# Layer 1's half tile taken by row in pairs, layer 2's loads issued in layer 1, and layer 1's last tiles closed between layer 2's first projections

## The chip, the cores and the metric

The kernel runs on one core of one Trainium2 chip, in one launch. The metric is the device time of that launch in microseconds (us); smaller is better. The core has five engines that run side by side, each through its own queue in order: PE (TensorE: matmuls and the loads of their weights, PEld), DVE (VectorE), ACT (ScalarE), POOL (GpSimd) and SP, whose queue here issues DMA transfers. Matmuls write to PSUM, which has eight banks of 512 fp32 columns by 128 partitions; DVE and ACT take the results out.

## The reference

Four layers follow each other on `x` of shape (4, 56, 56, 256), all in fp32, each after a normalisation and with the input added back: a 7x7 local attention (layer 0), a graph step over all tokens of an image (layer 1), a neighbourhood attention in two dilations (layer 2) and a shifted-window attention (layer 3). The change concerns layer 1, of which the reference is, cut to what matters:

```python
xn = x / maximum(norm(x, axis=-1), EPS)
A  = einsum('bnc,cc,bmc->bnm', xn, W_adj, xn)      # n = m = 3136 tokens
A  = exp(5.0 * (A - max(A))) * (1 - eye(n))
A  = A / sum(abs(A))
rowsum = sum(A);  xW = x @ W_aff.T
diff = rowsum * (xW + b_aff) - (A @ x) @ W_aff.T
y = (diff - mean(diff)) * rsqrt(var(diff) + LN_EPS) * ln_gamma + ln_beta
y = where(y > 0, y, 0.01 * y)
```

Only the diagonal of `W_adj` is used, so `A` before its row normalisation is symmetric: one block of exponentials serves the rows of one tile and, transposed, the rows of the other.

## The kernel before, in words

Activations lie channels first in DRAM, one buffer for each layer's input. `direct_blocks` runs `layer0` to `layer3` one after the other. Each layer opens its own memory pools (`early`, `big`, `pool`, `brief`, and one for PSUM), on alternate sides of SBUF, and closes them at its end. The program's order is an order of the text for PE in layer 1 and for all engines in layer 3 (`manual_schedule`); elsewhere a scheduler orders each engine's queue by its own estimate, and may lift an instruction out of a later layer as far as its memory and data allow.

**Layer 1** treats one image after the other. Its 3136 tokens make 24 tiles of 128 and a last one of 64 (tile 24, padded with zeros to 128). For each image the kernel keeps in SBUF `xnT` (unit-length tokens, channels on the partitions), `xw` (tokens times `W_aff`, with a column of -1 that yields the row sums) and `acc` (sums for tiles by column).

- `tokens` (L1346 to L1395) fills these four tiles (a chunk) at a time: `load` (DMA, normalise at L939, square on ACT at L1360), `lengths` (L1368), `values` (L1381, taken out by `evac` at L952 and L954) and `unit_length` (L1389, then L1391 on DVE). For the first image all seven chunks go through at once, loads two chunks ahead. For the next image each chunk is replaced while the present one no longer needs it, its steps spread between the units by a list `small`.
- The main loop goes through **units**: for each row block j = 0..24, groups of up to four tiles i >= j. A unit is `logits` (L1409: two accumulating matmuls of up to 512 columns; L1412: exp on ACT; on the diagonal a mask on POOL, L1414), `transposed` (L1423 on PE, L1426 on ACT) and `products`: for each tile a row product into `ps_o` (L1437, summed over the whole row block) and a column product into one of two `ps_v` buffers (L1442), which DVE adds to `acc` (L1446; the first time it copies, L1444). PE's order is: transposes of this unit, logits of the next, products of this one. An image has 91 units.
- When a row block is complete, `finish` (L1466 to L1489) adds both sums on DVE (L1473) and runs the layer normalisation over DVE and POOL; some units later `add` transposes the result back (L1494), adds it to the residual `xr` (L1502), takes statistics (L894) and writes the block out (L1505). After the last unit all remaining `add` steps run in a row.

**Layer 2** begins with `load(0)` (L1585), its weights `w_qkv` (L881), a bias table of 6.2 MB in two transfers (L1591), the exponential of half of that table in one ACT instruction (L1592), and then, for three row pieces, `prepare` (normalise, L939; the load of the next piece) and `project_rows` (value tiles L982, keys and queries L945). Its x tiles have two buffers. Value tiles go to DRAM and come back gathered (L1688) for the attention, whose logits (L1071) use 32 rows of the array each and whose products (L1100) use 32 columns each.

Of the kernel before, what the change touches and what calls it, by code (L numbers as in the profile page):

```python
# [31 lines left out]
NIMG = 4  # L32
# [798 lines left out]
def direct_blocks(ctx: ExitStack, tc: tile.TileContext, d: dict, watch):  # L831
# [499 lines left out]
    def layer1(early, big, pool, brief):  # L1331
        NB = -(-T // P)
        real = lambda i: min(P, T - i * P)
        nonlocal m_bufs
        m_bufs, ps_a = 1, ps_m
        w_aff = weight(early, "waff", C)
        acc = big.tile([P, NB, C + 1], FP, name="acc")
        xnT = big.tile([P, CC, NB * P], FP, name="xnT")
        xw = big.tile([P, NB, C + 1], FP, name="xw")
# [3 lines left out]
        nc.vector.memset(xw[T % P:, NB - 1, :], 0.0)  # L1343
        nc.vector.memset(xnT[:, :, T:], 0.0)

        def tokens(b, c, ps_a=ps_m):  # L1346

            tiles = range(4 * c, min(4 * c + 4, NB))
            n = sum(real(t) for t in tiles)
            k, m = real(tiles[0]), len(tiles)  # L1350
            box = {}

            def load():
                x = early.tile([P, CC, 512], FP, tag="x", name="x1")
                nc.sync.dma_start(out=x[:, :, :n], in_=tokens_of(1, b, 4 * c * P, n))
                x1 = box["x"] = early.tile([P, CC, 512], FP, tag="xn", name="xn1")
                sq = box["sq"] = early.tile([P, CC, 512], FP, tag="sq", name="sq", bufs=1)
                for h in range(CC):
                    normalise(x1[:, h, :n], x[:, h, :n], known(1, b), h)
                nc.scalar.activation(sq[:, :, :n], x1[:, :, :n], AF.Square)  # L1360

            def lengths():
                pm, sq = ps_a(), box["sq"]
                rn = early.tile([P, 4, 1], FP, tag="rn", name="rn")
                dg = box["dg"] = early.tile([P, 4, P], FP, tag="dg", name="dg", bufs=1)
                for i, t in enumerate(tiles):
                    for h in range(CC):
                        nc.tensor.matmul(pm[:k, i:i + 1], lhsT=sq[:, h, i * P:i * P + k], rhs=ones[:, 0:1],  # L1368
                                         start=(h == 0), stop=(h == CC - 1))
                nc.vector.tensor_scalar_max(rn[:k, :m, 0], pm[:k, :m], TINY * TINY)  # L1370
                nc.gpsimd.tensor_tensor(rn[:k, :m, 0], rn[:k, :m, 0], mhalf[:k, 0:1].to_broadcast([k, m]), ALU.pow)
                nc.gpsimd.tensor_tensor(
                    dg[:k, :m, :k], ident[:k, :k].rearrange("p (o q) -> p o q", o=1).to_broadcast([k, m, k]),
                    rn[:k, :m, :].to_broadcast([k, m, k]), ALU.mult)

            def values(i0):
                pm = ps_a()
                mm = min(2, m - i0)
                for i in range(i0, i0 + mm):
                    for h in range(CC):  # L1380
                        nc.tensor.matmul(pm[:k, (i - i0) * C:(i - i0 + 1) * C], lhsT=box["x"][:, h, i * P:i * P + k],  # L1381
                                         rhs=w_aff[:, h, :], start=(h == 0), stop=(h == CC - 1))
                evac(i0 // 2, xw[:k, 4 * c + i0:4 * c + i0 + mm, :C],
                     pm[:k, :mm * C].rearrange("p (a b) -> p a b", b=C))

            def unit_length():

                pm = ps_a()
                nc.tensor.matmul(pm[:, :n].rearrange("p (m k) -> p m k", k=k), lhsT=ones[:k, :], rhs=box["dg"][:k, :m, :k],  # L1389
                                 start=True, stop=True)  # L1390
                nc.vector.tensor_tensor(xnT[:, :, 4 * c * P:4 * c * P + n], box["x"][:, :, :n],  # L1391
                                        pm[:, :n].rearrange("p (o k) -> p o k", o=1).to_broadcast([P, CC, n]), ALU.mult)

            return [load, lengths] + [lambda i=i: values(i) for i in range(0, m, 2)] + [unit_length]

        xd, out, xr = {}, {}, {}

# [6 lines left out]
        def logits(b, j, first, last):  # L1404
# [10 lines left out]
            return e  # L1415

# [12 lines left out]
        def products(b, j, first, last, e, at):  # L1429
# [10 lines left out]
            def by_column(i):  # L1440
                pv = psum_tile("v", 2)
                nc.tensor.matmul(pv[:, :C + 1], lhsT=e[:, col(i)], rhs=xw[:, j, :], start=True, stop=True)  # L1442
                if j == 0:
                    nc.vector.tensor_copy(acc[:, i, :], pv[:, :C + 1])  # L1444
                else:
                    nc.vector.tensor_tensor(acc[:, i, :], acc[:, i, :], pv[:, :C + 1], ALU.add)  # L1446
# [10 lines left out]

        def residual(b, c):

            if (b, c) not in xr and c < NCH:  # L1460
                xr[b, c] = pool.tile([P, CC, CH], FP, tag="xr", name="xr1", bufs=3)
                nc.sync.dma_start(out=xr[b, c], in_=tokens_of(1, b, c * CH, CH))
            return xr.get((b, c))

        def finish(b, j):

            n = real(j)
            y = pool.tile([P, C + 1], FP, tag="y", name="y", bufs=5)
# [3 lines left out]
            if j:  # L1472
                nc.vector.tensor_tensor(y[:n], out[j][:n, :C + 1], acc[:n, j, :], ALU.add)  # L1473
            else:
                nc.vector.tensor_copy(y[:n], out[j][:n, :C + 1])
# [15 lines left out]
            def add():  # L1491
                pt = ps_a()
# [4 lines left out]
                while t0 < j * P + n:  # L1497
# [5 lines left out]
                    if t1 == (c + 1) * CH:  # L1503
# [7 lines left out]
        NC4 = -(-NB // 4)  # L1511
        units = [(b, j, i, min(i + 4, NB)) for b in range(NIMG) for j in range(NB) for i in range(j, NB, 4)]
        turn = iter(range(4 * NC4))
        fresh = [tokens(0, c, lambda: psum_tile(*(("v", 2), ("o", 2), ("t", 1), ("s", 2))[next(turn) % 4])) for c in range(NC4)]
        for c in range(2):
            fresh[c].pop(0)()
        for c in range(NC4):
            for step in fresh[c]:
                step()
            if c + 2 < NC4:  # L1520
                fresh[c + 2].pop(0)()
        scaled(0)
        e = logits(*units[0])
# [9 lines left out]
        def there(b, tile):  # L1533

            for item in [a for a in small if a[2] == (b, tile // 4)]:
# [3 lines left out]
        def replace(b, c):  # L1539
            load, *steps = tokens(b, c)  # L1540
            load()
            at = sum(a[2] is not None for a in small)
            small[at:at] = [(done + 8, step, (b, c)) for step in steps]

        for k, w in enumerate(units):
            b, j, first, last = w
            if first == j:
                residual(b, j * P // CH)
                residual(b, j * P // CH + 1)
                if b + 1 < NIMG and j % 4 == 2 and j >= 6:  # L1550
                    replace(b + 1, j // 4 - 1)
                if b + 1 < NIMG and j == NB - 1:
                    replace(b + 1, NC4 - 2)
                if b and j == 0:
                    replace(b, NC4 - 1)
            small_step()
            at = transposed(*w, e)
            if k + 2 < len(units) and units[k + 2][1] == units[k + 2][2]:
                scaled(units[k + 2][1])
            if k + 1 < len(units):  # L1560
                there(units[k + 1][0], units[k + 1][3] - 1)
                ahead = logits(*units[k + 1])
            small_step()
            products(*w, e, at)
            done += last - first
            if last == NB:
                small.append((done + 6, finish(b, j), None))
            e = ahead
        for _, step, _ in small:
            step()  # L1570
# [5 lines left out]
    def layer2(early, big, pool, brief):  # L1576
        nonlocal m_bufs
        m_bufs = 2
        (types1, w1), (types2, w2) = window_types(S), window_types(G2)
        xs, xns, q, attns, ahead = {}, {}, {}, {}, []  # L1580
# [5 lines left out]

        load(0)
        w_qkv = weight(early, "wqkv2", 3 * C)
        bias = early.tile([P, 4, w1 + w2], FP, name="bias2", bufs=1)
        for a in (1, 0):  # L1590
            nc.sync.dma_start(out=bias[:, 2 * a:2 * a + 2, :], in_=d["bias2"][:, 2 * a:2 * a + 2, :])  # L1591
        nc.scalar.activation(bias[:, 2:4, :], bias[:, 2:4, :], AF.Exp)  # L1592
# [164 lines left out]
        for i in range(3):  # L1757
            prepare(i + 1)
            for step in project_rows(i):
                step()  # L1760
        attend_pairs(pool, stream())
# [193 lines left out]
    for l, layer in enumerate((layer0, layer1, layer2, layer3)):  # L1955
        side = "left" if l % 2 == 0 else "right"
        with tc.tile_pool(name=f"d{l}e", bufs=2, side=side, reuse_waits="tile") as early, \
                tc.tile_pool(name=f"d{l}", bufs=1, side=side, reuse_waits="tile") as big, \
                tc.tile_pool(name=f"d{l}w", bufs=2, side=side, reuse_waits="tile") as pool, \
                tc.tile_pool(name=f"d{l}l", bufs=2, side=side, reuse_waits="tile") as brief, \  # L1960
                tc.tile_pool(name=f"dpsum{l}", bufs=2, space=PSUM, reuse_waits="tile") as ps:
            E = mybir.EngineType
            fixed = {layer1: {E.PE}, layer3: {E.PE, E.DVE, E.Activation, E.Pool}}.get(layer)
            order = tc.manual_schedule(engines=fixed) if fixed else nullcontext()
            with order:
                layer(early, big, pool, brief)
# [99 lines left out]
```

## Time and profile before

| | us |
|---|---|
| three timed runs | 4103.39, 4103.79, 4105.45 (median 4103.79) |
| the profiled execution | 4092.52 |
| its span, first to last instruction | 4090.7 |
| mean granted PE clock | 0.979 |
| layer 1's steady part | about 850 to 2826 |
| layer 2's first projection | starts at 2845.9 |

The profile has, beside its page, the order of time of every engine, what each waited for, and busy times by stretch. Times in it count from the start of the span. "Busy" of PE is the union of its matmuls, each shown with its latency, so that the distance between two starts is the better price of a matmul. A merged row (x4) stands for that many instructions in a row; a matmul of fp32 operands appears as two, a transposition as one. The granted clock is the share of its full rate that PE was given.

### The profile page before, as it was taken

What the parts mean: (1) busy time and instruction counts of PE and PEld (TensorE: products, weight loads), DVE (VectorE), ACT (ScalarE), POOL (GpSimd) and SP (SyncE); (2) the same over time, 40 slices, a digit from 0 to 9 for tenths busy, and PEclk for the clock granted to TensorE, in tenths of its full rate; (3) what the DMA queues carried; (4) which work ended last, traced back from release to release, by engine and by line L of the source; (5) the groups of instructions that cost most, each with busy time, mean ns of one, the idle gap of its engine ahead of it and who ended that gap; (6) DMA issues with size and microseconds to landing.
All of it is one profiled execution on the core that took longest, in us unless ns stands there. A gap on an engine that the chain in (4) does not pass through costs nothing. (4 is left out here: it accounts for less than half of the span.)

```text
span 4090.7 us, 92322 instructions
## 1 busy us (share of the span) xinstructions
PE 3889.7 (95%) x39031; PEld 2778.1 (68%) x39031; DVE 2369.5 (58%) x4445; ACT 1377.7 (34%) x2890; POOL 1741.9 (43%) x1883
## 2 busy tenths in 40 slices
PE   7899999899999999999999999997999999999998
PEld 4566666577777677776777767775676766666665
DVE  6777777634445444454344543444688877666665
ACT  3445555322222122222222212222555555444443
POOL 2576767621123211242112421123677777554544
PEclk9899999899999999999999999998999999999999
DMA  7344333210000100001000000002344443322221
GB/s 259 101 136 126 116 116 104 90 32 10 15 15 24 34 10 15 15 24 34 10 15 15 23 23 9 10 19 108 108 135 124 131 118 111 108 72 73 73 75 63
DMA packets 239986, 275.88 MB, mean 67 GB/s; under 512 B 22342, under 2 KB 231912, under 8 KB 239080
## 3 DMA queue, kind: packets, MB, share of 16 engines
q1 hardware_dynamic: 239274, 269.80, 21.0%
q8 instruction: 309, 5.06, 0.5%
q14 instruction: 115, 0.94, 0.1%
q10 hardware_dynamic: 288, 0.08, 0.0%
HBM read 190.29 MB, written 79.53 MB: 66 GB/s over the span
## 5 line engine op out<-in xcount | busy, mean ns | idle before, releaser
L1446 DVE TENSOR_TENSOR acc<-acc,ps_v 128x257 f32<-128x257 f32 x1104 | 457.7, 421 | 679.2 <-PE ps_v L1442 676.5
L1442 PE MATMUL ps_v<-xw,e 128*128 128x257 f32 x2400 | 666.6, 382 | 27.2 <-DVE acc L1446 17.2
L1437 PE MATMUL ps_o<-xw,at 128*128 128x257 f32 x2400 | 663.2, 380 | 0.0
L1409 PE MATMUL ps_s<-xnT,xd 128*128 128x512 f32 (+3 forms) x1456 | 622.9, 550 | 5.1 <-DVE xnT L1391 5.1
L1442 PEld LDWEIGHTS ps_v<-xw,e 128*128 128x128 f32 x2400 | 445.0, 189 | 193.2 <-issue 91.8
L1426 ACT COPY at<-ps_t 128x512 f32<-128x512 f32 (+3 forms) x360 | 184.8, 513 | 1053.7 <-PE ps_t L1423 1053.7
L1091 POOL TENSOR_TENSOR b<-e 126x336 f32<-126x336 f32 (+5 forms) x512 | 499.7, 997 | 11.6 <-ACT e L1079 3.6
L1437 PEld LDWEIGHTS ps_o<-xw,at 128*128 128x128 f32 x2400 | 455.9, 190 | 65.5
L1402 POOL TENSOR_SCALAR xd<-xnT,vec 128x128 f32<-128x128 f32 x200 | 122.2, 622 | 707.4 <-PE ps_s L1409 705.6
L945 PE MATMUL ps_m<-xn,w_wqkv 128*128 128x392 f32 x1024 | 380.1, 505 | 2.7 <-DVE xr L1729 2.7
L1082 POOL TENSOR_TENSOR e<-e,m0t 126x672 f32<-126x672 f32 (+3 forms) x128 | 239.3, 1870 | 271.1 <-ACT e L1081 229.6
L1409 PEld LDWEIGHTS ps_s<-xnT,xd 128*128 128x128 f32 x1456 | 245.1, 191 | 155.6 <-issue 138.8
L1082 POOL TENSOR_TENSOR e<-e,bias 119x784 f32<-119x784 f32 (+5 forms) x128 | 244.6, 1911 | 202.0 <-ACT e L1081 200.8
L1412 ACT ACTIVATE e<-ps_s 128x512 f32<-128x512 f32 (+3 forms) x364 | 200.8, 552 | 376.7 <-PE ps_s L1409 376.0
L1003 ACT ACTIVATE no<-rs 128x168 f32<-128x168 f32 (+2 forms) x256 | 93.8, 367 | 596.2 <-DVE rs L1694 271.7
L945 PEld LDWEIGHTS ps_m<-xn,w_wqkv 128*128 128x128 f32 x1024 | 189.4, 192 | 126.1 <-ACT pr L1922 17.5
L1100 PEld LDWEIGHTS ps_o<-e,vp 124*32 124x32 f32 (+3 forms) x8192 | 176.9, 111 | 142.3 <-issue 94.8
L1100 PE MATMUL ps_o<-e,vp 124*32 124x112 f32 (+3 forms) x8192 | 239.5, 254 | 6.1 <-POOL e L1082 4.5
L939 DVE TENSOR_SCALAR xn<-x,gst 128x28 f32<-128x28 f32 (+5 forms) x368 | 206.1, 614 | 56.4 <-PE ps_m L945 27.7
L1079 ACT ACTIVATE e<-e 126x672 f32<-126x672 f32 (+5 forms) x256 | 219.5, 857 | 19.2 <-DVE e L1078 6.2
L1694 DVE RECIPROCAL rs<-ps_o 128x196 f32<-128x196 f32 (+2 forms) x128 | 176.0, 1375 | 78.8 <-PE ps_o L1100 78.3
L1032 POOL TENSOR_TENSOR e<-e,m3l 98x784 f32<-98x784 f32 x64 | 118.2, 1847 | 236.1 <-ACT e L1029 236.1
(169 smaller groups left out, 6176.6 us busy)
## 6 DMA issues: line engine op xcount, KB each, us to landing
x<-xr SPq DMA_DIRECT2D x64, 392.0 KB
x<-in_x SPq DMA_DIRECT2D x53, 448.0 KB
xr<-x SPq DMA_DIRECT2D x60, 392.0 KB
x<-x SPq DMA_DIRECT2D x60, 392.0 KB
vd<-v SPq DMA_DIRECT2D x48, 384.0 KB
xr<-in_x SPq DMA_DIRECT2D x32, 392.0 KB
xr<-x SPq DMA_DIRECT2D x28, 448.0 KB
x<-xr SPq DMA_DIRECT2D x28, 448.0 KB
```

What stands on the lines that cost most here:

```text
L939: nc.vector.tensor_scalar(dst, src, gst[:, h, 0:1], gst[:, h, 1:2], ALU.subtract, ALU.mult)
L945: nc.tensor.matmul(pm[:, :n], lhsT=w[:, h, col:col + P], rhs=rhs(h), start=(h == 0), stop=(h == CC - 1))
L1079: nc.scalar.activation(ev, ev, AF.Exp)
L1082: nc.gpsimd.tensor_tensor(parts(ev), parts(ev), w["emask"], ALU.mult)
L1091: nc.gpsimd.tensor_tensor(w["b"][a][:nk, :, :2 * nq].rearrange("p h (i c) -> p h i c", i=2), ev[:, :, :, 0, :], ev[:, :, :, 1, :], ALU.add)
L1100: nc.tensor.matmul(w["o"](k, i)[j * HD:(j + 1) * HD], lhsT=ones[:nk, :HD] if k else v(j, u), rhs=w["b"][j // 2][:nk, j % 2, i * nq:(i + 1) ...
L1409: nc.tensor.matmul(s[:, :n], lhsT=xd[j][:, h, :], rhs=xnT[:, h, first * P:last * P], start=(h == 0), stop=(h == CC - 1))
L1412: nc.scalar.activation(e[:, :n], s[:, :n], AF.Exp, scale=5.0)
L1426: nc.scalar.copy(at[:, sl], pt[:, sl])
L1437: nc.tensor.matmul(out[j][:, :C + 1], lhsT=e[:, col(i)] if i == j else at[:, col(i)], rhs=xw[:, i, :], start=(i == j), stop=(i == NB - 1))
L1442: nc.tensor.matmul(pv[:, :C + 1], lhsT=e[:, col(i)], rhs=xw[:, j, :], start=True, stop=True)
L1446: nc.vector.tensor_tensor(acc[:, i, :], acc[:, i, :], pv[:, :C + 1], ALU.add)
```

## The change

**The half tile.** Tile 24 leaves the row blocks: j and i now run over 24 tiles, and the blocks of an image make 84 units. The half tile is treated as a row of its own, in three units (q = 0, 1, 2) of eight tiles each. The last chunk of tokens loads the 64 tokens twice, so that they stand on partitions 0 to 63 and 64 to 127, and POOL scales them into `xdr`. In a unit, the logits of the 64 tokens with tiles 8q..8q+3 go to partitions 0 to 63 of `ps_s`, those with 8q+4..8q+7 to partitions 64 to 127; one exp, four transposes and one copy serve both halves. Then, four times, two column products that read 64 partitions each, into both `ps_v` buffers, and two row products that write 64 partitions each of one `ps_o`; `racc` sums the row products over the three units. For the first image units 0 and 1 come first and unit 2 after block 0; for a later image units 0 and 1 come after blocks 20 and 21 of the image before, unit 2 after its own block 0. A column sum is copied into `acc` when touched first, on DVE or (second half) on ACT, and added by DVE otherwise.

**Chunks.** The squares are written over the loaded x instead of into a buffer of their own, and the chunks of the next image are replaced at blocks 3, 6, 10, 14, 18, 20 and 22.

**The layer boundary.** Layer 2's `early` pool is opened before layer 1's pools. `layer2_ahead`, with `load(0)`, `w_qkv`, the bias table and its exponential in six pieces, is called inside layer 1 (text position: third image, block 8; the queues' own order sets when it is issued). The pool with `y` and `xr` (`late`) lives on into layer 2, and the `add` steps still open at the end of layer 1 are returned and run one by one after each step of layer 2's second and third `project_rows`.

```diff
+        def rest_logits(q):
+            s = psum_tile("s", 2)
+            for a in range(2):
+                for h in range(CC):
+                    nc.tensor.matmul(s[a * REST:(a + 1) * REST, :], lhsT=xdr[:, h, a * REST:(a + 1) * REST],
+                                     rhs=xnT[:, h, (2 * q + a) * 512:(2 * q + a + 1) * 512], ...)
+            e = pool.tile([P, 512], FP, tag="e", name="e1", bufs=3)
+            nc.scalar.activation(e, s, AF.Exp, scale=5.0)
...
+        def rest_products(b, q, e, own, at):
+            po = psum_tile("o", 2)
+            for i in range(4):
+                pv = [psum_tile("v", 2) for a in range(2)]
+                for a in range(2):
+                    half = slice(a * REST, (a + 1) * REST)
+                    nc.tensor.matmul(pv[a][:, :C + 1], lhsT=e[half, i * P:(i + 1) * P], rhs=xw[half, NB, :], ...)
+                for a in range(2):
+                    add_up(b, 8 * q + 4 * a + i, pv[a], (nc.vector.tensor_copy, nc.scalar.copy)[a])
+                for a in range(2):
+                    nc.tensor.matmul(po[a * REST:(a + 1) * REST, :C + 1], lhsT=at[:, i * P + a * REST:i * P + (a + 1) * REST],
+                                     rhs=xw[:, 8 * q + 4 * a + i, :], ...)
+            if own is not None:
+                nc.tensor.matmul(po[:REST, :C + 1], lhsT=own, rhs=xw[:REST, NB, :], start=False, stop=True)
...
-                sq = box["sq"] = early.tile([P, CC, 512], FP, tag="sq", name="sq", bufs=1)
+                sq = box["sq"] = x
...
+                if c == NC4:
+                    for h in range(CC):
+                        nc.gpsimd.tensor_scalar_mul(xdr[:, h, :], xnT[:, h, NB * P:], adj[:, h:h + 1])
...
-        for _, step, _ in small:
-            step()
+        return [step for _, step, _ in small]
...
+        def exponential(h, i):
+            part = bias[:, h, i * (w1 + w2) // 3:(i + 1) * (w1 + w2) // 3]
+            nc.scalar.activation(part, part, AF.Exp)
...
             for step in project_rows(i):
                 step()
+                if i and last_steps:
+                    last_steps.pop(0)()
```

In the changed kernel the matmuls of the half tile stand at L1443 (logits), L1451 and L1479 (its own 64 by 64 block), L1462 (transposes), L1472 (column products) and L1476 (row products); full tiles at L1421, L1491, L1505 and L1510, the adds to `acc` at L1433, the closing transposes at L1562.

## The prediction

> **What bounds the kernel now.** I read the page's first two parts first, for the engine that is always busy, then the order of time on TensorE (PE) for the price of one step, then the stretches around the end of layer 1.
>
> ```profile
> PE 3889.7 (95%) x39031; PEld 2778.1 (68%) x39031; DVE 2369.5 (58%) x4445; ACT 1377.7 (34%) x2890; POOL 1741.9 (43%) x1883
> ...
> PE   7899999899999999999999999997999999999998
> ...
> PEclk9899999899999999999999999998999999999999
> ```
>
> PE is busy 95% of the span, in every slice but the first and the one after layer 1; no other engine passes 58%. In layer 1 (850 to 2826 us) PE is busy 1935.2 of 1976 us, DVE 860. What leaves PE there leaves the time. Now PE alone, in one full unit of layer 1 (start, length, engine, line; "x4" counts merged instructions):
>
> ```profile
> 1410.44 0.60 PE L1423 MATMUL ps_t<-ident,e 128*128 128x128 f32 x4
> 1410.87 1.88 PE L1409 MATMUL ps_s<-xnT,xd 128*128 128x512 f32 x4
> 1412.59 1.03 PE L1442 MATMUL ps_v<-xw,e 128*128 128x257 f32 x4
> 1413.46 0.60 PE L1437 MATMUL ps_o<-xw,at 128*128 128x257 f32 x2
> ...
> 1415.19 1.03 PE L1437 MATMUL ps_o<-xw,at 128*128 128x257 f32 x4
> 1416.06 0.49 PE L1423 MATMUL ps_t<-ident,e 128*128 128x128 f32 x3
> ```
>
> Starts, not lengths, give the price, because matmuls overlap by their latency. 1410.44 to 1416.06 is 5.62 us for four tile pairs, 1.405 us each: transposition 0.108, logits 0.43, column product 0.433, row product 0.433. Each matmul is two passes, each costing 0.843 ns a column (0.43 us for 512). Units follow with no gap.
>
> The end of layer 1 (length, then busy time with counts for PE, PEld, DVE, ACT and POOL, then the granted PE clock and DMA):
>
> ```profile
> 2826.00:2846.00 20.00, 2.25 (x9) 1.11 (x9) 11.25 (x35) 0.20 (x1) 6.70 (x10) 0.58 0.52 183
> 2846.00:2857.00 11.00, 10.57 (x36) 6.49 (x36) 1.12 (x2) 4.34 (x10) 0.00 (x0) 0.83 0.98 422
> 2857.00:2865.00 8.00, 0.00 (x0) 0.00 (x0) 0.27 (x1) 4.11 (x2) 0.00 (x0) 0.69 0.77 281
> ```
>
> PE does 2.25 us of work in 20, then layer 2's first projection, then nothing for 8, while the clock falls to 0.58. The waits name it: closing transposes for y (5.0 us) and xr (5.7), the w_qkv transfer (7.1), the second xn (8.7).
>
> **Part 1, the half tile.** Before, tile 24 costs one pair in each of 24 row blocks and its own: 24 x 1.405 + 0.88 = 34.6 us an image. After, three units an image take eight tiles each, in 64-row or 64-column halves. In line: logits 8 passes of 512 (3.46), four transposes (0.43), products 32 passes of 257 (6.93), three times over, plus 0.65 for the tile's own: 33.1 us. Almost nothing is saved unless two halves run at once. No row has 64-wide pairs; the nearest are layer 2's 32-wide ones:
>
> ```profile
> 2928.90 0.97 PE L1100 MATMUL ps_o<-e,vp 124*32 124x112 f32 x32
> 2929.69 0.57 PE L1100 MATMUL ps_o<-b,ones 124*32 124x112 f32 x16
> 2930.19 1.12 PE L1071 MATMUL ps_s<-q,kI 32*126 32x84 f32 x32
> 2931.24 1.58 PE L945 MATMUL ps_m<-xn,w_wqkv 128*128 128x392 f32 x4
> ```
>
> 32 passes of 112 columns would be 3.02 us in line; the next group starts 0.79 later: four at a time. The single records start in fours, as far apart as one pass. That holds for column groups (L1100) and row groups (L1071), so I take two at once for products: 3.47 a unit. Logits differ: each half's four passes stand together in the order, so the second half must start past the first one's queue. Ends: 4 slots of 0.43 or 8; I take 6, their middle, 2.59. Paired: 3 x (2.59 + 0.43 + 3.47) + 0.65 = 20.1 us.
>
> Changing the array's shape costs time. From the end of a group's last stream to the next effective start (its modelled end less latency and columns), medians here are: full to column groups 0.117 (L945 to L1100), 0.143 where L982 goes to a 64-wide last tile, back 0.195; full to row groups 0.163 (four cases), row to column 0.126, column to row 0.168 to 0.191; within a shape nothing. A unit has 0.34 around the logits and 0.163 + 4 x 0.126 + 3 x 0.18 + 0.195 = 1.40 in the products: 1.74, three times, plus 0.13 for the own product: 5.4. So 25.5 against 34.6: 9.1 an image, 36.4 us in all.
>
> Two rules of the Trainium skill speak against this. "TensorE: Matmul & The Clock Gate", Part 3, The mechanism, says matmuls start in strict program order; logits would then overlap in one slot only, 7 instead of 6: an estimate of 5.2 us less gain. The same part, under Measured speedup, gives four row tiles 3.07 times, not 4; at that share the products' pairs would cost an estimate of 12 us more. L1100's 0.79 us shows no such loss.
>
> New waits: a pair needs both ps_v buffers. In the first two units of an image the columns are first touched and copied by DVE (0.42) and ACT side by side: 0.43 stream + 0.2 latency + 0.42 + 0.1 is 1.15, the 1.17 that PE needs per step; hidden. In the third, both go through DVE's adds (L1446, 0.421): 1.56 against 1.17, 0.39 x 4 steps x 4 images = 6.2 us. Queued behind a waiting pair are the row product and the next unit. DVE's in-order queue adds more: L1442 idles 27.2 us over 1200 products today, and 48 pairs each wait for two buffers: about 4 (0 to 12). Net of part 1: 26.4.
>
> **Part 2, layer 1's start.** The first logits now wait for the half tile's chain: xnT (0.3), then two POOL scalings (0.62 each, L1402's row), about 2 us; before, L1409 followed L1389 in 0.36. The two bias transfers (6.2 MB) are now queued on SP between the first image's chunk loads, and in ACT's order three of the six exponentials (0.87 each, a sixth of the 5.2 us of L1592) stand before the fifth chunk's square. The 8 MB queued at the boundary moved in some 25 us, so 3.1 MB is about 9.6 us; loads run two chunks (12.2 us) ahead: mostly hidden. Ends 0 and 10, I take 2. Cost of this part: 4.
>
> **Part 3, image ends.** Today's shrinking blocks (4, 3, 2, 1 tiles) outrun DVE and POOL: PE is busy 15.2 of 20 us at 1842 and at 2348, 5.9 of 10 at 1335 with a clock of 0.51 in the next ten. After, two units of 8 us stand between these blocks, but two short blocks still end it. Gain 4 (-5 to 15).
>
> **Part 4, the boundary.** Before, from the last product (2825.9) to the third projection (2875.84) is 49.9 us. After: the order puts layer 2's first projection straight behind the last product; its x, weights and bias have landed long before. What is late next is DVE: xn's second half stands ten instructions behind the last block's y, among waits for POOL. By today's tail (last y 3.2 us after the product, its statistics at 6.5) about 6 us. Then two projections 2 x (12 x 0.217 + 16 x 0.33) = 15.8, five closing transposes 1.1, four short row-group insertions 2.2, and 2 for a lowered clock (today's first 12 passes took 4.7 instead of 2.6): 27.1. Gain 22.8 (12 to 28). SP's x loads stand behind xr and before vd; each lands some 4 us after its buffer is free, under the 7.9 us projection ahead of it. If that cover went, 8.7 us as today. Closings now lie beside projections and cost DVE only.
>
> Behind this point PE's order equals the old one; layers 2 and 3 keep their time.
>
> **Sum.** 26.4 - 4 + 4 + 22.8 = 49.2 us. The profiled execution took 4092.5 (span 4090.7), which gives 4043; it is 11.3 below the median of the runs, 4103.8. Against the median: 4055.
>
> **Rivals.**
> - *Everything overlaps* (logits in 4 slots, 10.4 more; no DVE stall beyond the adds, 4; image ends well filled, 8): 4033. For it: groups of four show no loss. Against: no row has several passes of one half queued ahead of the other.
> - *The boundary stays open:* xn late behind POOL's waits, or the second x held behind SP's queue, returning today's 8.7 wait and some 12 us of the first: 4076. For it: DVE and SP are in order. Against: both x buffers are free early.
> - *Slower, the halves run in line:* at the paired steps (L1443, L1472, L1476 of the change) each half waits for the other. Logits lose 2 slots x 0.43 x 12, products 41.6: 52 us; with a shape drain between halves (108 x 0.17) 70: 4107 to 4125, taken 4115. It decides once some 70% of the pairs do so. For it: no 64-wide pair in this trace. Against: both 32-wide kinds overlap fully.
> - *Nothing moves:* PE saves, but another engine sets layer 1's pace. DVE is at 44% there; I give it 0.03.
>
> **Numbers.** Forecast 0.66 (own range 4040 to 4072), everything overlaps 0.12, boundary open 0.12, in line 0.07, nothing moves 0.03. Two measurements of this kernel can tell 0.2% (8 us) from no change. Faster by more: the first three less a little, 0.88; within: 0.05; slower: 0.07. The range leaves out the last two cases and the farthest ends: 4030 to 4083.
>
> **What will show it.** Half-tile products: 16 passes of L1472 and 16 of L1476 in about 5 us a unit confirm pairs and shapes, about 8.4 refute them; logits' four slots show as 1.7, in line 3.5. Stalls appear as waits of L1472 on L1433 or DVE. The boundary: last L1505 to third L982 group near 27 us. If layer 1's first 60 us grow by over 10, the bias transfers were not hidden. I am wrong if layer 1 is not shorter by 15 to 45 us, or the boundary by 12 to 28.

## The result, and the profile after

The changed kernel takes 4049.3 us (median of 4 runs, 4046.8 to 4066.1) against 4104.6 for the kernel before beside it: 0.9874 of the time, 95% interval 0.9850 to 0.9898. 4055 was forecast. The sum was nearly right, its terms were not: two large ones were wrong in opposite directions.

The profiled executions (us). "Start" is the first lengths pass of layer 1, "layer 1" from there to its last product, "boundary" from there to layer 2's third projection, "behind" the rest of the span; "half clock" is the time lost in layer 1 because the granted clock stood at 0.5, taken as half the length of those stretches. That is an estimate: it counts the waits inside them too (3.2 us after, by waits of over 0.15 us), but the layer 1 of act_copies and of products_in_line below comes out with it.

| kernel | start | layer 1 | boundary | behind | half clock |
|---|---|---|---|---|---|
| before | 809.2 | 2016.4 | 50.3 | 1214.8 | 6.8 |
| before, a second profile | 813.7 | 2016.3 | 50.1 | 1218.1 | 6.8 |
| after | 800.2 | 2002.2 | 31.2 | 1211.0 | 30.7 |
| change | -9.0 | -14.2 | -19.1 | -3.8 | +23.9 |
| forecast | 0 | -26.4 | -22.8 | 0 | 0 |

The first part of the page after (busy time, share, count) and two rows of its 40 slices:

```profile
PE 3858.0 (95%) x38983; PEld 2715.6 (67%) x38983; DVE 2364.8 (58%) x4427; ACT 1375.9 (34%) x2899; POOL 1741.2 (43%) x1883
...
PE   6999999899999999999999999999999999999998
...
PEclk9899999899999999999999999999999999999999
```

PE is as full as before, and the gap behind layer 1 no longer shows in a slice. On this scale the low clock cannot be seen either. A half-tile unit of the changed kernel, PE alone, at full clock and without a wait:

```profile
863.52 0.63 PE L1462 MATMUL ps_t<-ident,e 128*128 128x128 f32 x4
863.99 1.88 PE L1421 MATMUL ps_s<-xnT,xd 128*128 128x512 f32 x4
865.80 0.70 PE L1472 MATMUL ps_v<-xw,e 64*128 64x257 f32 x4
866.44 0.65 PE L1476 MATMUL ps_o<-xw,at 128*64 128x257 f32 x4
...
869.46 0.70 PE L1472 MATMUL ps_v<-xw,e 64*128 64x257 f32 x4
870.09 0.65 PE L1476 MATMUL ps_o<-xw,at 128*64 128x257 f32 x4
870.68 0.55 PE L1491 MATMUL ps_t<-ident,e 128*128 128x128 f32 x3
```

From 865.80 to 870.68 is 4.88 us for 32 passes; the forecast was 3.47 + 1.40 = 4.87. By this the pairs run fully at once (products_in_line below shows it). The logits of a later unit:

```profile
1317.70 1.94 PE L1443 MATMUL ps_s<-xnT,xdr 128*64 128x512 f32 x8
1319.58 0.70 PE L1505 MATMUL ps_o<-xw,e 128*128 128x257 f32 x2
```

1.88 us from start to start, less about 0.15 for the change of shape, is four slots (a slot is the 0.43 us of one 512-column pass), not six. The single records start in twos, 13 ns apart, then 0.43 us later the next two. But the same products behind another block:

```profile
1324.84 0.70 PE L1472 MATMUL ps_v<-xw,e 64*128 64x257 f32 x4
1325.47 0.66 PE L1476 MATMUL ps_o<-xw,at 128*64 128x257 f32 x4
1327.73 0.70 PE L1472 MATMUL ps_v<-xw,e 64*128 64x257 f32 x4 [1.60 <-DVE acc L1436]
1328.36 0.71 PE L1476 MATMUL ps_o<-xw,at 128*64 128x257 f32 x4
1329.79 1.23 PE L1472 MATMUL ps_v<-xw,e 64*128 64x257 f32 x4 [0.73 <-DVE acc L1436]
1330.95 1.13 PE L1476 MATMUL ps_o<-xw,at 128*64 128x257 f32 x4
1332.01 1.23 PE L1472 MATMUL ps_v<-xw,e 64*128 64x257 f32 x4
```

After two waits for DVE, 0.70 becomes 1.23: these passes run at half speed although nothing waits any more. The stretches around it (length, busy time and count of PE, PEld, DVE, ACT, POOL, then the granted clock):

```profile
1320.00:1330.00 10.00, 7.67 (x42) 4.67 (x42) 5.79 (x16) 3.25 (x6) 4.21 (x7) 0.94 0.00 0
1330.00:1340.00 10.00, 10.00 (x38) 5.64 (x40) 1.44 (x4) 1.12 (x3) 1.85 (x2) 0.50 0.06 15
1340.00:1350.00 10.00, 10.00 (x42) 6.76 (x38) 3.70 (x10) 2.15 (x4) 1.87 (x4) 0.88 0.00 1
```

PE is "10.00 busy" in the second row, and half of that is the clock. The busy column hides it; only the clock column tells. PE's longest waits in layer 1 after (total, times, longest):

```profile
PE ps_v L1510 <- DVE acc L1433: 18.0, 25, 1.5
PE ps_v L1472 <- DVE acc L1436: 11.7, 9, 1.6
PE ps_v L1472 <- DVE acc L1433: 8.5, 8, 2.1
PE ps_v L1376 <- ACT x L1368: 3.4, 1, 3.4
```

Why DVE is late, in the unit at 1408 (DVE alone):

```profile
1408.54 0.41 DVE L1554 TENSOR_SCALAR y<-y,mv,rstd 128x256 f32<-128x256 f32 x1 [0.68 <-POOL rstd L1553]
1408.87 0.15 DVE L922 TENSOR_SCALAR dv<-ps_m 128x2 f32<-128x2 f32 x1
1408.94 0.41 DVE L1433 TENSOR_TENSOR acc<-acc,ps_v 128x257 f32<-128x257 f32 x1
1411.14 0.66 DVE L1557 SCALAR_TENSOR_TENSOR y<-y 128x256 f32<-128x256 f32 x1 [1.79 <-POOL y L1556]
1411.72 0.74 DVE L1433 TENSOR_TENSOR acc<-acc,ps_v 128x257 f32<-128x257 f32 x2
```

The last step of the finished block's y waits 1.79 us for POOL, and the add that would free `ps_v` stands behind it. Ten of the twelve half-tile units follow the end of a block closely and have such a wait of 1.6 to 2.1 us; the first two units of the first image, with no block ahead of them, have none.

The boundary after (rows as above), and its first waits:

```profile
2803.00:2823.00 20.00, 15.18 (x46) 9.31 (x46) 10.96 (x32) 3.74 (x12) 6.82 (x10) 0.74 0.38 119
2823.00:2834.00 11.00, 9.92 (x54) 5.74 (x49) 5.33 (x14) 3.03 (x10) 0.00 (x0) 1.00 0.40 131
```

```profile
PE ps_m L982 <- DVE xn L939: 3.7, 1, 3.7
PE ps_m L945 <- DVE v L986: 1.2, 2, 0.8
PE ps_m L982 <- DVE mv L1551: 0.6, 1, 0.6
```

PE works 15 of the first 20 us instead of 2.25; the waits for y, xr, w_qkv and the second xn are gone.

### The profile page after: what moved, and what is told of

Same layout as the page of the kernel before. It is cut to its first block, busy times and chain, and to the rows that moved or that the text cites. A ratio compares the mean times of both kernels' runs of the same rounds, so it can differ in the third digit from the quotient of the medians.

```text
span 4044.6 us, 92225 instructions
## 1 busy us (share of the span) xinstructions
PE 3858.0 (95%) x38983; PEld 2715.6 (67%) x38983; DVE 2364.8 (58%) x4427; ACT 1375.9 (34%) x2899; POOL 1741.2 (43%) x1883
## 4 chain that ended last, share of the span: by engine, by line
PE 48%; DVE 4%; POOL 2%; issue 1%; SPq 0%; DMA 0%; ACT 0%; DVEq 0%; POOLq 0%; ACTq 0%
PE ps_m L945 12%; PE ps_o L1505 6%; PE ps_s L1421 6%; PE ps_v L1510 6%; PE ps_o L1100 3%; PE ps_m L962 3%; PE ps_s L1071 3%; PE ps_o L1040 2%; PE ps_m L982 2%; PE ps_t L1491 1%; PE ps_s L1025 1%; DVE rs L1796 1%; PE ps_m L1389 1%; DVE xn L939 0%; DVE e L1078 0%
## 5 line engine op out<-in xcount | busy, mean ns | idle before, releaser
L1433 DVE TENSOR_TENSOR acc<-acc,ps_v 128x257 f32<-128x257 f32 x1104 | 455.8, 421 | 686.5 <-PE ps_v L1510 671.7
L1510 PE MATMUL ps_v<-xw,e 128*128 128x257 f32 x2208 | 613.1, 382 | 19.7 <-DVE acc L1433 18.0
L1505 PE MATMUL ps_o<-xw,at 128*128 128x257 f32 x2208 | 609.0, 379 | 0.0
L1421 PE MATMUL ps_s<-xnT,xd 128*128 128x512 f32 (+3 forms) x1344 | 571.1, 547 | 0.0
L1494 ACT COPY at<-ps_t 128x512 f32<-128x512 f32 (+3 forms) x332 | 170.5, 514 | 1049.8 <-PE ps_t L1491 1049.8
L1510 PEld LDWEIGHTS ps_v<-xw,e 128*128 128x128 f32 x2208 | 408.6, 189 | 171.1 <-issue 80.4
L1505 PEld LDWEIGHTS ps_o<-xw,at 128*128 128x128 f32 x2208 | 419.1, 190 | 60.1
L1421 PEld LDWEIGHTS ps_s<-xnT,xd 128*128 128x128 f32 x1344 | 225.5, 191 | 134.8 <-issue 126.2
L1424 ACT ACTIVATE e<-ps_s 128x512 f32<-128x512 f32 x336 | 185.3, 551 | 336.7 <-PE ps_s L1421 336.7
```

The costliest lines, as they stand in the source:

```text
L1421: nc.tensor.matmul(s[:, :n], lhsT=xd[j][:, h, :], rhs=xnT[:, h, first * P:last * P], start=(h == 0), stop=(h == CC - 1))
L1424: nc.scalar.activation(e[:, :n], s[:, :n], AF.Exp, scale=5.0)
L1505: nc.tensor.matmul(out[j][:, :C + 1], lhsT=e[:, col(i)] if i == j else at[:, col(i)], rhs=xw[:, i, :], start=(i == j), stop=(i == NB - 1))
```

## The experiments

**My theory after seeing this:** the pairs work; what the change lost, it lost to DVE's in-order waits and to the half clock that follows each of them. **Rivals:** the halves themselves lower the clock; the two adds per step are the price; the loads at layer 1's start are.

Each ratio is against the kernel before beside the same runs. Its medians were 4099.9 us beside half_alone, boundary_alone and closings_back, 4095.2 beside the four runs from act_copies to bias_late, and 4091.4 beside the rest, so ratios of different groups are not compared; what an edit is worth is read from its stretches. Among the four, half_chunk_first (4051.7), which changes nothing, can stand for the changed kernel.

**Parts apart.** The half tile alone has the boundary of the kernel before, and the squares in a buffer of their own, so that layer 2's loads go late again:

```diff
-                sq = box["sq"] = x
+                sq = box["sq"] = early.tile([P, CC, 512], FP, tag="sq", name="sq", bufs=1)
...
-                if (b, j) == (NIMG - 2, 8):
-                    small += [(done + 20, step, None) for step in next_layer()]
...
-        return [step for _, step, _ in small]
+        for _, step, _ in small:
+            step()
+        return []
```

> Only the half tile's pairs; the loads of layer 2, its bias table and the closings stand at the layer boundary as in the kernel before. The forecast's sizes: layer 1 shorter by 26.4 + 4 - 2 = 28 us, so about 4076. Second theory, that each wait of over 1.4 us in a half-tile unit also halves the granted clock for one to four stretches of 3.4 us: first product step to last product shorter by only 14 to 20 us, about 4085 to 4091, with half-clock stretches of 17 us or more behind such waits at the ends of the first three images. The boundary should stay at 48 to 52 us by both.

4070.2 us, 0.9930 (0.9907 to 0.9952). Start 810.2, layer 1 1995.6, boundary 48.1, behind 1214.9, half clock 29.0. Layer 1 is 20.8 us shorter, between both numbers and near the second; 29.0 us of half clock against 6.8 is the second theory's mark. The times (4062.7 to 4075.1) alone do not decide: their median lies below both.

The boundary alone has the layer 1 of the kernel before, with `xr` and `y` from the pool that lives on, `sq = x`, the call of `next_layer` and the returned steps.

> Only the boundary: layer 1 computes the half tile as the kernel before does, but layer 2's loads stand in layer 1 and the closings amid the projections. The forecast's sizes: boundary 27 instead of 50 us, layer 1's start 2 us later, so about 4084. If the loads at the start of layer 1 are not hidden (in the changed kernel one wait of 3.4 us on ACT's square stands there), the start costs 4 to 9 and the time is 4088 to 4092. By the changed kernel's trace the boundary is 31 us.

4079.0 us, 0.9952 (0.9935 to 0.9969). Start 802.3, layer 1 2023.2, boundary 33.3, behind 1218.3. The boundary is 17 us shorter; layer 1 is 6.8 longer, within the unhidden loads' 4 to 9; the start is 7 to 11 us earlier, which neither expectation had. The two parts add up: 0.70% and 0.48% are 1.18% of the 1.26%, each known to about 0.2%; in layer 1, 20.8 less and 6.8 more are 14.0 of the 14.2.

> The changed kernel, but the open steps of layer 1 are closed at its end instead of amid the projections. If the moved closings bring most of the boundary's gain, the boundary goes from 31 back to 43 or more and the time from 4049 to about 4061. If the early loads bring it, under 5 us are lost: 4049 to 4054, and PE waits for DVE's y ahead of the first projection only as long as it does now.

Edit: the last step of the first diff alone, loads early as in the change. 4058.3 us (0.9913, 0.9881 to 0.9945), between the two expectations; its four times lie in two pairs at 4048 and 4069, so the stretch decides: boundary 32.5 against 31.2 after. The moved closings are worth 1.3 us at most (the half clock in the two stretches differs by 1.7); the early loads bring the rest (48.1 to 32.5).

> The kernel before, once more, for a second profile. If the 9 us by which layer 1 began earlier in the changed kernel's profile came from the change, layer 1's first lengths start at 809 us again; if they are the clock's own variation between executions (five half-clock stretches fewer in layer 0), the start moves by several us, to anywhere between 798 and 812.

Start 813.7: 4.5 us later than in the first profile, so two profiles of one kernel differ by half of the 9 us. But over all profiles the three kernels that load layer 1's first chunk early start at 809.2 to 813.7, the ten others (without the last experiment) at 797.6 to 805.6. In the former, DVE normalises and ACT squares that chunk amid layer 0 (at 367 us in the kernel before); in the latter, layer 2's pools take the room, and ACT squares it at 792 to 800 us.

**The stalls.** Both first-touch copies go to ACT:

```diff
-                    add_up(b, 8 * q + 4 * a + i, pv[a], (nc.vector.tensor_copy, nc.scalar.copy)[a])
+                    add_up(b, 8 * q + 4 * a + i, pv[a], nc.scalar.copy)
```

> The changed kernel, but in the half-tile units both first-touch copies of the column sums go to ACT, none to DVE. First theory, waits of TensorE on DVE also halve the granted clock: the waits of 1.6 us in the units at the ends of the first three images go, and the eight half-clock stretches of 3.4 us that begin behind them with them; layer 1 shorter by 5.5 + 13.6 = 19 us (2002 to 1983). Rival, the low clock comes from the 64-wide halves themselves: only the waits go, 5 to 6 us, and the half-clock stretches at 1329 to 1342, 1851 and 2329 to 2342 stay. Third: ACT, in order too, becomes what the pairs wait for, with no gain.

4032.7 us, 0.9857 (0.9834 to 0.9880). Layer 1 is 16.4 us shorter (1985.8), with 10.2 less half clock. L1472 waits 11.0 us instead of 20.2. The waits of L1472 in layer 1 (the first line is the third unit's):

```profile
PE ps_v L1472 <- DVE acc L1433: 8.5, 8, 2.1
...
PE ps_v L1472 <- ACT acc L1436: 2.5, 2, 1.3
```

The same units as at 1324 above, now 1.7 us earlier:

```profile
1320.00:1330.00 10.00, 10.00 (x62) 6.10 (x60) 3.89 (x11) 4.08 (x11) 4.22 (x7) 1.00 0.01 2
1330.00:1340.00 10.00, 10.00 (x50) 7.24 (x49) 3.86 (x11) 2.44 (x5) 3.41 (x5) 1.00 0.06 13
```

The halves are the same, the wait is gone, and the clock stays at 1.00: the rival that halves alone lower the clock falls. An undisturbed unit takes 5.3 instead of 4.88, since ACT copies both; that is the price. By these sizes 9.2 less waiting and 10.2 less half clock, for eight units longer by 0.42, give 16.0 of the 16.4.

The third unit of an image moves into block 1:

```diff
-                if j == 0:
-                    units.append((b, None, 2))
+                if j == 1:
+                    units.insert(-3, (b, None, 2))
```

> The changed kernel, but the third half-tile unit of an image stands amid block 1 instead of right behind block 0, away from the finishing steps of a block on DVE. First theory: its four waits of 1.6 to 2.3 us on DVE (7.9 us) go, and the half-clock stretches that begin behind them (five of 3.4 us, 8.5 us) with them: layer 1 shorter by some 16 us. Rival, the low clock comes from the half units themselves: 8 us at most, and the stretches move along with the unit. Third, the price is the two DVE adds per step (0.39 us times 16): nothing changes.

4025.7 us, 0.9837 (0.9818 to 0.9856). Layer 1 is 19.1 us shorter (1983.1), of that 10.2 half clock. The third unit, 8.9 to 10.8 us long before up to the products of its own block (L1479), is undisturbed in all four images:

```profile
1420.85 0.70 PE L1472 MATMUL ps_v<-xw,e 64*128 64x257 f32 x4
1421.49 0.65 PE L1476 MATMUL ps_o<-xw,at 128*64 128x257 f32 x4
1422.07 1.02 PE L1472 MATMUL ps_v<-xw,e 64*128 64x257 f32 x4
1423.03 0.65 PE L1476 MATMUL ps_o<-xw,at 128*64 128x257 f32 x4
1423.61 0.70 PE L1472 MATMUL ps_v<-xw,e 64*128 64x257 f32 x4
...
1426.37 0.65 PE L1479 MATMUL ps_o<-xw,own 64*64 64x257 f32 x2
```

1420.85 to 1426.37 is 5.5 us for the four steps, two adds in each. The first step takes 1.22 us as in a unit without adds, the second 1.54, and so on in turn: the adds cost 0.64 us a unit, not 1.56.

**Layer 1's start.** The chunks are taken in the order half tile, then 0 to 5 (`fresh = fresh[NC4:] + fresh[:NC4]`):

> The changed kernel, but the first image's half-tile chunk is prepared first of the seven instead of last, so that its scaled copy is ready long before the first logits. If the chain of that chunk costs what its waits show (POOL's dg 2.3, POOL's xdr 1.4, then three half-clock stretches, 5.1), layer 1 is shorter by 4 to 9 us. By the forecast's size of this chain, 2 us. If another chunk's chain stands in the same place, nothing.

4051.7 us (0.9901, 0.9878 to 0.9925), layer 1 2002.3: nothing. Waits for ACT's square at the start grow from 3.4 to 5.3 us while those for POOL shrink; another chain stands in the same place.

```diff
         for a in (1, 0):
+            nc.vector.tensor_copy(bias[:, 2 * a:2 * a + 2, 0], src[:, 0, 0:2])
             nc.sync.dma_start(out=bias[:, 2 * a:2 * a + 2, :], in_=d["bias2"][:, 2 * a:2 * a + 2, :])
```

> The changed kernel, but the two bias transfers wait for a value that is written in the third image, so that they and the six exponentials leave layer 1's start (4 numbers more are copied on DVE). By the forecast 2 us of layer 1's start go. By the changed kernel's trace the wait of 3.4 us on ACT's square and one half-clock stretch go: 3 to 7 us. If the loads of x were what is late at the start, and not ACT, up to 10.

(`src` is `xnT`.) 4048.4 us (0.9891, 0.9872 to 0.9910), layer 1 1998.6: 3.6 us shorter. The wait of 3.4 on ACT is gone, the half clock is not less (32.4).

**All edits that helped**, the two stall edits and the late bias:

> The changed kernel with three edits at once: first-touch copies on ACT, the third half-tile unit amid block 1, and the bias transfers held back to the third image. If the waits and the clock add up as they were measured alone (layer 1 shorter by 16.4, 19.1 and 3.6 us), layer 1 takes 1963 us and the time is about 4010. If the low clock of one place only moves to the next, 4020 to 4026, the time of the better edit alone.

4008.8 us, 0.9798 (0.9778 to 0.9818), faster than both kernels. Layer 1 takes 1962.6 us where 1963 was expected, with 10.2 of half clock. The waits of L1472 in it are down to one row:

```profile
PE ps_v L1472 <- ACT acc L1436: 2.5, 2, 1.3
```

The half clock that is left begins in five places. One is layer 1's start, behind a wait of 2.27 us for POOL; two follow these waits for ACT; and two (1324.4 and 2307.4) follow no wait of over 0.15 us, but the lengths passes of the next image's chunk, of one column each:

```profile
1321.73 0.65 PE L1476 MATMUL ps_o<-xw,at 128*64 128x257 f32 x4
1322.31 1.95 PE L1376 MATMUL ps_m<-ones,x 128*128 128x1 f32 x16
```

In act_copies the same passes stand behind the same unit (at 1328.45), and the clock stayed at 1.00.

**What the pairs are worth.** Products ordered so that no two halves stand side by side:

```diff
-            for i in range(4):
-                pv = [psum_tile("v", 2) for a in range(2)]
-                for a in range(2):
-                    half = slice(a * REST, (a + 1) * REST)
+            for a, i0 in ((0, 0), (0, 2), (1, 0), (1, 2)):
+                half = slice(a * REST, (a + 1) * REST)
+                pv = [psum_tile("v", 2) for i in range(2)]
+                for i in (i0, i0 + 1):
```

> The changed kernel, but the products of a half-tile unit are ordered so that no two halves stand side by side: two column products of one half, then its two row products, first half before second; as many changes of shape as before. If the two halves of a pair run fully at once, an undisturbed unit grows from 4.88 us by 16 passes of 0.217, 3.47, to 8.35; the disturbed units (7.2 to 10.8 us) grow by less, since DVE has more time. In all 25 to 42 us longer: 4074 to 4091. If the pairs saved less than they seem to, an undisturbed unit grows by clearly less than 3.47.

An undisturbed unit (PE alone):

```profile
857.71 1.13 PE L1472 MATMUL ps_v<-xw,e 64*128 64x257 f32 x4
858.77 1.08 PE L1476 MATMUL ps_o<-xw,at 128*64 128x257 f32 x4
859.78 1.13 PE L1472 MATMUL ps_v<-xw,e 64*128 64x257 f32 x4
...
866.00 0.38 PE L921 MATMUL ps_m<-dv,group 128*128 128x2 f32 x2
```

8.29 us, 3.41 more, as expected from pairs that run fully at once. But the kernel takes only 4060.0 (0.9922, 0.9899 to 0.9945), and layer 1 13.2 more, below my 25: the half clock is 13.7 instead of 30.7, and L1472 waits 9.9 us instead of 20.2. 41 of longer work, less 17 of half clock, less 10 of waits, is 14. So in the changed kernel as it stands, two thirds of what the pairs save is given back.

> The changed kernel, with the eight logits passes of a half-tile unit ordered by 128 channels and then by half, instead of by half first. If the order in the program sets which passes run at once, this order has to bring four slots (1.72 us), and the order by half first would need seven or eight; the changed kernel's trace shows passes of both halves starting 13 ns apart in the other order already. If the order does not matter, the eight passes take four slots in both, and layer 1 stays at 2002 us within 4.

Four slots in both orders, the halves 7 ns apart instead of 13; layer 1 1999.3, in one run. The order does not matter. PE's queue had the order of the text in both, as far as the first unit tells: POOL is late there with the second part of `xdr` (written by 849.17 us, swapped 857.33). In the swapped kernel the weight loads of four passes start before that; by half first only two do, and the other half's stand behind.

```diff
                 x = early.tile([P, CC, 512], FP, tag="x", name="x1")
+                if b == 0 and c < 2:
+                    nc.sync.dma_start(out=x[:, :, :1], in_=tokens_of(1, NIMG - 1, T - 1, 1))
                 nc.sync.dma_start(out=x[:, :, :n], in_=tokens_of(1, b, 4 * c * P, n))
```

> The kernel before, but the first two chunks of layer 1 are loaded only when layer 0 has stored its last tokens, as the changed kernel does for want of room (each load waits for a small transfer that is overwritten). If the loss of this early load is what starts layer 1 some 10 us earlier in the kernels with early loads of layer 2, layer 1's first lengths stand at 809 to 814 us instead of 820 to 825, and layer 1 itself takes 3 to 8 us more: 0 to 8 us faster in all. If that difference is chance, the start stays at 820 to 825 and the time grows by 3 to 8.

The expectation counts from some 11 us before the span's start: in the span's time it gave 798 to 803 or 809 to 814. Start 805.4 is between the two: layer 0's last matmul ends at 794.2 instead of 809.3, but then PE waits 11.2 us for the late chunk. Layer 1 is 2022.5, 6.1 longer. The time is 4102.6 against 4091.4, 1.0027 (1.0016 to 1.0039): slower by more than either theory had. That layer 0 ends earlier without the early chunk is shown in profiles; that this gains time is not.

## Why the prediction was right, and which steps failed

By the prediction's own last sign ("I am wrong if layer 1 is not shorter by 15 to 45 us, or the boundary by 12 to 28"), layer 1 just misses with 14.2 us, and the boundary is inside with 19.1. The parts show why.

**Part 1, streaming: right, better by one term.** Counting each pass as its columns times 0.843 ns and a pair once, layer 1 streams 1901.9 us before and 1833.7 after: 68.2 less, where the forecast's pairs give (34.6 - 20.1) x 4 = 58.0. The missing 10.2 is the logits: four slots instead of the six I took as the middle of 4 and 8 (10.4 by the forecast's own rival). The Trainium skill, "TensorE: Matmul & The Clock Gate", Part 3, The mechanism, has matmuls start in strict program order; the four slots of the unswapped order disagree with that here. The same part, under Measured speedup, has 3.07 times for four row tiles; a loss of that kind does not show in the pairs of this case, whose products save 3.41 of 3.47.

**Shapes, waits, start and ends: right in sum only.** What is neither streaming nor clock grows by 30.1 us (107.7 to 137.8); the forecast has 21.6 for shapes, 10.2 for DVE, 4 for the start, -4 for the ends, 31.8. (With them part 1 is 36.4 - 6.2 - 4 = 26.2 net; the 26.4 of the prediction is a slip of 0.2.) The shape price is confirmed by the 4.88. L1472's waits are 20.2, twice the forecast: the adds, priced 6.2, cost 0.64 a unit where nothing else is late, some 2.6, and the other DVE item, "DVE's in-order queue adds more: ... about 4 (0 to 12)", is nearly all of it. It was priced from the average over all products, but the units stand where DVE's queue is worst. The start's 2 us for hidden transfers is 3.6 (bias_late), with 6.8 for the whole move of loads (boundary_alone); from the first lengths pass to the first logits it takes 48.3 us instead of 40.4, 7.9 where part 2 had 4, of it 2.1 half clock. The ends gained more than 4: three rows of waits of the kernel before, for DVE's `mv` behind a block, POOL's `e` and `xnT`,

```profile
PE ps_v L1442 <- DVE mv L1483: 8.9, 3, 3.0
PE ps_o L1437 <- POOL e L1414: 5.3, 6, 1.3
PE ps_s L1409 <- DVE xnT L1391: 5.1, 6, 1.3
```

19.3 us in all, are 2.0 after (L1510 on `mv` 1.7, L1505 on `e` 0.3). But L1472's new waits stand at the same ends. With the forecast's shapes, 21.6 + 20.2 + 5.8 - 17.3 = 30.3 by these rows, an estimate near the 30.1.

**The failed step: no clock in part 1.** The prediction priced a wait as the wait. Its own text showed a clock of 0.51 behind 4 us of idling at an image end, and used a lowered clock only at the boundary. Layer 1 lost 30.7 us to it instead of 6.8. With it the change of layer 1 is -68.2 + 30.1 + 23.9 = -14.2 (the 30.1 is what is left over, so it is the estimate above, and the experiments, that support the split). Act_copies and unit2_later show that taking the waits away takes much of the clock loss along. The 10.2 us left in the combined kernel begin at layer 1's start, behind two waits for ACT and behind one-column passes; no edit took these away.

**Part 4: mechanism right, size off by the same term.** 31.2 instead of 27.1. Projections and closings stream 16.94 us and the row-group insertions take 1.84 from start to start, together 18.8 (forecast 15.8 + 1.1 + 2.2 = 19.1); the half clock is 5.1 (forecast 2), the rest 7.3, of it 3.7 the wait for xn (forecast 6). The closings' place, for which the prediction had no price of its own, is worth 1.3 at most.

**Not forecast: 9.0 ahead of layer 1 and 3.8 behind it.** "Layers 2 and 3 keep their time" holds to about what two profiles of one kernel differ by (1214.8 and 1218.1; over all fourteen 1207.5 to 1218.9). The 9.0 may in part be such variation (4.5 between two profiles of the kernel before), and goes with the first chunk's early load, a transfer that the change moved out of layer 0 and that the prediction did not see. Ahead of layer 1 the half clock takes 34.1 us after, 42.7 and 49.5 in the two profiles before, so most of the 9.0 shows there; why it is less was not tested. Whether the later load is a net gain stays open.

**The rivals.** "Everything overlaps" was right on the logits and wrong on the stalls. "The halves run in line" is refuted by the 4.88 us; its price of 41.6 for the products would also have been too high: 13.2 in layer 1. By the terms I was right in the total through two errors of 10 and 24 us in layer 1, and 13 us from elsewhere.

## What to carry to other kernels

Ask of every new wait on TensorE whether it also brings the clock down, and read the clock column beside the busy column: waits of 1.60 and 0.73 us were followed by some 13.7 us of half clock here, 6.8 us more (sixteen one-column passes lie in the same stretch). Count passes of few columns with the waits. Put short or half-filled work where the engine that frees its buffers is not in the midst of a chain that waits for a third engine; the average wait per product tells nothing about that place. When a pool is moved, look for the transfers that lose the room that it takes.

## What the runs showed of the hardware

The low clock comes in stretches of 3.41 us (or several), which start on one grid. In the fourteen profiles of this case, take for each such stretch at full clock that lies wholly in layer 1 the share in which PE streams columns (0.843 ns each, from a pass's start on, a pair counted once, a 1-column pass as one column). Where the share was under 0.36, the next stretch was at half clock in 46 of 46 cases; from 0.36 to 0.48 in 43 of 92; above 0.48 in 0 of 7888. The counts move by some ten with the place at which a pass is taken to stream; what decides between 0.36 and 0.48 is open. So no full stop is needed. An undisturbed half-tile unit streams 3.47 of 4.88 us, 0.71, because of its changes of shape, and a full unit nearly 1: by these shares it can bear less waiting before it falls under the line (the 1.75 us at 1314.7 to 1316.5 in the kernel before left a share of 0.41, and no low clock followed). The Trainium skill, "TensorE: Matmul & The Clock Gate", HAM oscillation, warns of idle gaps over some 3.4 us; here a wait of 1.6 us in one stretch was enough at 1849 us of the changed kernel, and no wait of over 0.15 us stood in front of 1324.4 us of the combined one.
